# Expert blocks ordered by their first row's batch, with finished batches summed between the blocks

## The chip, the cores and the metric

The kernel runs on one core of one Trainium2 chip. The metric is device microseconds of one execution. Four runs of the kernel before gave a median of 751.23 us, between 750.31 and 752.97. A profile is one further execution with the hardware profiler on, and it has its own time.

The engines are written as in the profile: PE (TensorE), DVE (VectorE), ACT (ScalarE), POOL (GpSimd) and SP (SyncE, which here only issues DMAs). SPq, ACTq, POOLq are the engines' instruction queues.

## What is computed

One adaLN transformer block on x of 4 batches, 512 tokens each, 256 wide, in float32: a gated attention part and a gated mixture of experts. The part that matters here is the second one:

```python
h = _layernorm(x) * (1 + cb) + sb
cw = _combine_weights(h, gate_w)        # 4 of 16 experts per token, weights that sum to 1
out = 0
for e in range(16):
    a = _swiglu(h @ expert_up_w[e].T)   # 256 -> 2 x 176 -> 176
    out = out + cw[:, e:e + 1] * (a @ expert_down_w[e].T)
out = out + _swiglu(h @ shared_up_w.T) @ shared_down_w.T
x = x + gb * out                        # gb: a gate per batch and column
```

Only the 4 chosen experts of a token have a weight other than zero. The 2048 tokens give 8192 (token, expert) rows.

## The kernel before

**Routing.** `attention()` works through the batches in order. When a batch is done, the routing picks each token's four experts, and 16 indirect DMAs on POOL (L1342) write its rows into `rows_d` in DRAM. `rows_d` has a region of 2176 rows for each expert; a row holds the 256 values, the token's number and its 16 weights. `free` (16 numbers, L250) is where each expert's region is filled to; `slots` (L1325 to L1339) hands out the places and moves it on (L1333). Since batches are routed in order, the rows of an expert stand in the order of their batches.

**Table.** When all four batches are routed, `make_table` (L314) works out on DVE which 128 rows each of `NBLK` = 79 blocks takes: from the counts it gets the number of blocks per expert (L322, L329), the first block of each (L334, L338), and then, in five operations of 79 x 16 = 1264 columns on all partitions (L345, L352, L356, L365, L369), the expert and the row of every block. All partitions hold the same table; the blocks lie along the free axis, ordered by expert. SP and PE read a block's row and expert from partition 0 into a register (`read`, L388).

**Shared expert.** `shared` (L397) runs for all tokens around the table. Its up products are L416 on PE, L427 on ACT and L435, L436 on DVE; its down product is L454 on PE, then L464 on DVE (tile `o`, two buffers) and L470 on POOL, which adds it to `x_sb`.

**Blocks.** `block(j)` takes the rows of one block: `fetch` (L1493, a DMA issued by SP, into one of seven `x` buffers), `turn` (L1504, PE transposes), `copy` (L1509, ACT), `meta` (L1514 and L1517 on DVE: the token numbers, and the rows' weights for this expert, picked out with the table's `is_of` by a product and a reduce), `up` (L1524, PE), `silu` (L1534, ACT), `product` (L1538, DVE), `turn_back` (L1543, PE), `copy_back` (L1547, DVE), `down` (L1552, PE), `weigh` (L1562, ACT, into one of five `y_b` buffers), and `put` (L1565): an indirect DMA on POOL that adds the 128 rows to `acc_d` in DRAM by token. There are two arrays `acc_d`; block j adds to number j % 2, so a put waits for the put two blocks earlier.

**End.** After all blocks, the eight halves of batches are loaded from both arrays (L1613: one array on SP, one on ACT), added (L1618), multiplied by the gate (L1619), added to `x_sb` (L1623, on POOL and DVE in turn) and stored (L1624).

**What sets the order.** PE, DVE, ACT and SP run their instructions in the order in which `Plan` (L83) emits them. Every piece is added with an engine, a cost in us, its needs, and a due time; `Plan.next` takes the operation that can start first by these costs, and the lower due time among equals. `hold` models the buffers (`takes`, `gives`). The program then waits on semaphores for what each instruction reads and writes; DRAM tiles are tracked too, apart from `rows_d`. An engine's queue goes strictly in order.

Of the kernel before, what the change touches and what calls it, by code (L numbers as in the profile page):

```python
# [10 lines left out]
F32 = mybir.dt.float32  # L11
# [6 lines left out]
P = 128  # L18
# [18 lines left out]
CAP = B * S + P  # L37
NBLK = B * S * TOPK // P + E - 1
# [113 lines left out]
def kernel(  # L152
# [92 lines left out]
    tile_rows = steps_of("tile_rows", [P, B * NT], [[P, B * NT]])  # L245
    number = steps_of("number", [P, NBLK], [[1, NBLK]])
    expert = steps_of("expert", [P, E], [[1, E]])
    begin = steps_of("begin", [P, E], [[CAP, E]])

    free = const.tile([P, E], F32, name="free")  # L250
    nc.gpsimd.tensor_copy(free, begin)
# [59 lines left out]

    table = {}

    def make_table(pool, needs, due):  # L314
        t, n = table, NBLK

        def counts():

            rows = pool.tile([P, E], F32, name="rows", bufs=1)
            nc.vector.tensor_tensor(rows, free, begin, ALU.subtract)  # L320
            full = pool.tile([P, E, B * NT], F32, name="full", bufs=1)
            nc.vector.tensor_tensor(  # L322
                full,
                rows.unsqueeze(2).to_broadcast([P, E, B * NT]),
                tile_rows.unsqueeze(1).to_broadcast([P, E, B * NT]),
                ALU.is_gt,
            )
            t["blocks"] = pool.tile([P, E], F32, name="blocks", bufs=1)
            nc.vector.tensor_reduce(t["blocks"], full, AX.X, ALU.add)  # L329

        def starts():
            blocks = t["blocks"]
            earlier = pool.tile([P, E, E], F32, name="earlier", bufs=1)
            nc.vector.tensor_tensor(  # L334
                earlier, before, blocks.unsqueeze(1).to_broadcast([P, E, E]), ALU.mult
            )
            first = t["first"] = pool.tile([P, E], F32, name="first", bufs=1)
            nc.vector.tensor_reduce(first, earlier, AX.X, ALU.add)  # L338
            t["last"] = pool.tile([P, E], F32, name="last", bufs=1)
            nc.vector.tensor_tensor(t["last"], first, blocks, ALU.add)  # L340

        def of():

            t["gone"] = pool.tile([P, n, E], F32, name="gone", bufs=1)
            nc.vector.tensor_tensor(  # L345
                t["gone"],
                t["last"].unsqueeze(1).to_broadcast([P, n, E]),
                number.unsqueeze(2).to_broadcast([P, n, E]),
                ALU.is_le,
            )  # L350
            t["of"] = pool.tile([P, n], F32, name="of", bufs=1)
            nc.vector.tensor_reduce(t["of"], t["gone"], AX.X, ALU.add)  # L352

        def is_of():
            t["is_of"] = pool.tile([P, n, E], F32, name="is_of", bufs=1)
            nc.vector.tensor_tensor(  # L356
                t["is_of"],
                expert.unsqueeze(1).to_broadcast([P, n, E]),
                t["of"].unsqueeze(2).to_broadcast([P, n, E]),
                ALU.is_equal,  # L360
            )

        def base():

            nc.vector.tensor_tensor(  # L365
                t["gone"], t["is_of"], t["first"].unsqueeze(1).to_broadcast([P, n, E]), ALU.mult
            )
            t["row"] = pool.tile([P, n], F32, name="row_f", bufs=1)
            nc.vector.tensor_reduce(t["row"], t["gone"], AX.X, ALU.add)  # L369
            nc.vector.tensor_tensor(t["row"], number, t["row"], ALU.subtract)  # L370

        def rows():

            row, of = t["row"], t["of"]
            nc.vector.tensor_scalar(row, row, float(P), None, ALU.mult)
            nc.vector.scalar_tensor_tensor(row, of, float(CAP), row, ALU.mult, ALU.add)
            nc.vector.tensor_scalar(row, row, float(E * CAP), None, ALU.min)
            nc.vector.tensor_scalar(of, of, float(E - 1), None, ALU.min)
            for name in ("row", "of"):
                t[f"{name}_i"] = pool.tile([P, n], mybir.dt.int32, name=f"{name}_i", bufs=1)  # L380
                nc.vector.tensor_copy(t[f"{name}_i"], t[name])

        op = needs
        for f, cost in ((counts, 0.9), (starts, 0.9), (of, 2.8), (is_of, 1.4), (base, 2.8), (rows, 1.0)):
            op = plan.add("DVE", cost, f, needs=[op], due=due)
        return op

    def read(t, n, engine, top):  # L388
        return nc.values_load(
            t[0:1, n : n + 1],  # L390
# [97 lines left out]
    def attention():  # L488
        with ExitStack() as ectx:
# [665 lines left out]
            def norm2(b, adds, due):  # L1155
# [165 lines left out]
                def slots():  # L1321
# [7 lines left out]
                        free.unsqueeze(1).to_broadcast([P, NT, E]),  # L1329
# [3 lines left out]
                    nc.vector.tensor_tensor(free, free, pc[:, NT, :], ALU.add)  # L1333
# [100 lines left out]
    def ffn():  # L1434
# [5 lines left out]
        SP, PE = mybir.EngineType.SP, mybir.EngineType.PE  # L1440
# [19 lines left out]
        for b in range(EARLY_SHARED, B):  # L1460
# [5 lines left out]
            "DVE", 0.2, lambda: nc.vector.tensor_copy(ends, free), [routed[B - 1]["slots"]], 60.0  # L1466
        )

        def blanks(e):
            r = read(ends, e, SP, E * CAP - P)  # L1470
# [12 lines left out]
        def block(j):  # L1483
            st = {}
            due = 300.0 + j
            names = ("x", AHEAD + 1), ("pt2", 2), ("xt", 2), ("token", 6), ("pu", 2), ("sg", 2), \
                ("a_b", 2), ("pb", 1), ("at_b", 2), ("py", 2), ("y_b", 5)
            h = {name: hold(name, bufs) for name, bufs in names}

            def fetch():  # L1490
                r = read(t["row_i"], j, SP, E * CAP)
# [9 lines left out]
            def turn():  # L1501
# [3 lines left out]
                st["e"] = read(t["of_i"], j, PE, E - 1)  # L1505
# [4 lines left out]

            def meta():
                x = st["x"]
                st["token"] = fp.tile([P, 1], mybir.dt.uint32, name="token", bufs=6)
                nc.vector.tensor_copy(st["token"], x[:, D : D + 1])  # L1514
                st["cw"] = fp.tile([P, 1], F32, name="cw_b", bufs=6)
                junk = fp.tile([P, E], F32, name="junk")
                nc.vector.tensor_tensor_reduce(  # L1517
                    junk, x[:, D + 1 :], t["is_of"][:, j, :], 1.0, 0.0, ALU.mult, ALU.add, st["cw"]
                )
# [40 lines left out]
            def weigh():  # L1560
                st["y"] = fp.tile([P, D], F32, name="y_b", bufs=5)
                nc.scalar.activation(st["y"], st["py"], AF.Copy, scale=st["cw"])  # L1562

            def put():
# [12 lines left out]
            xt = plan.add("ACT", 0.37, copy, [op], due - 1.4, takes=[h["xt"]], gives=[h["pt2"]])  # L1577
            me = plan.add(
                "DVE", 0.4, meta, [fe, op], due - 0.3, takes=[h["token"]], gives=[h["x"]]
# [11 lines left out]
            )  # L1591
            op = plan.add("PE", 0.87, down, [op], due + 1.1, takes=[h["py"]], gives=[h["at_b"]])
# [3 lines left out]
            plan.add(  # L1596
                "POOL", 1.56, put, [op], due + 1.1, lag=4.0, gives=[h["y_b"], h["token"]]
            )

        for j in range(NBLK):  # L1600
            block(j)
# [5 lines left out]

        half = NT // 2
        sums = []
        for n in range(B * NT // half):  # L1610
            pair = [ep.tile([P, half, D], F32, name=f"s{n}_{i}") for i in range(2)]
            for t, acc, eng in zip(pair, acc_d, (nc.sync, nc.scalar)):
                eng.dma_start(  # L1613
                    out=t, in_=acc[ts(n, half * P), :].rearrange("(n p) d -> p n d", p=P)
# [70 lines left out]
```

## Time and profile before

| | |
|---|---|
| median of four runs | 751.23 us (750.31 to 752.97) |
| the profiled execution | 754.97 us |
| its span, first to last instruction | 753.0 us |
| granted PE clock, mean | 0.943 |
| busy: PE, DVE, ACT, POOL | 656.4, 455.6, 317.9, 347.1 us |

By stretch of the span (us from its start; busy us of each engine; the granted clock; the mean busy share of the 16 DMA engines):

| stretch | what runs | PE | DVE | ACT | POOL | PE clock | DMA |
|---|---|---|---|---|---|---|---|
| 50 to 430 | attention, routing of three batches | 353.87 | 286.06 | 206.82 | 171.60 | 0.97 | 0.24 |
| 430 to 463 | last batch, weights of the experts arrive | 28.53 | 19.54 | 4.88 | 12.07 | 0.97 | 0.87 |
| 463 to 488 | table, shared expert, last scatters | 12.42 | 14.69 | 1.42 | 18.48 | 0.75 | 0.65 |
| 488 to 536 | shared expert, first blocks | 47.52 | 20.14 | 11.55 | 13.27 | 0.96 | 0.23 |
| 536 to 717 | blocks | 181.00 | 66.30 | 84.12 | 112.33 | 1.00 | 0.67 |
| 717 to 726 | last blocks drain | 2.59 | 0.84 | 1.41 | 4.68 | 0.92 | 0.59 |
| 726 to 753 | sums and stores | 0.00 | 16.97 | 0.00 | 6.23 | 0.50 | 0.70 |

How to read the profile's lines. In a timeline a line is: start, duration, engine, source line, operation, out<-in, shapes, how many were merged (x), and in brackets how long the engine had been idle before and what released it. A group of a source line gives the count and the shortest, median and longest duration in ns, then the first and last start. "issue" as a releaser means that the profile shows nothing that the engine waited for. The ends of PE's operations are modelled.

### The profile page before, as it was taken

Reading aid. Unit: us, or ns where it says so; the run is one execution under the profiler, and the core shown is the slowest. Engines: PE = TensorE matmul, PEld = TensorE weight load, DVE = VectorE, ACT = ScalarE, POOL = GpSimd, SP = SyncE. Lnnn points to the kernel's source line nnn. Section 1 sums busy time; section 2 is a strip of 40 time slices with the busy share of each in tenths; the row PEclk is TensorE's granted clock in tenths of the full one; section 3 lists DMA queues with packets and bytes.
Section 4 is the critical chain, followed back from the end, with each engine's and each line's share of the span. In section 5 each row is a group of like instructions: output and inputs, shape, how many; then the busy total and the mean of one; then the engine's idle time right before and its main releaser. Section 6 shows DMA issues by size and latency. Waiting matters only on the chain.

```text
span 753.0 us, 12881 instructions
## 1 busy us (share of the span) xinstructions
PE 656.4 (87%) x4205; PEld 413.4 (55%) x4236; DVE 455.6 (61%) x1286; ACT 317.9 (42%) x557; POOL 347.1 (46%) x449
## 2 busy tenths in 40 slices
PE   6577999999999999999988895599999999999920
PEld 3343455554544544545543484488777777777710
DVE  4685868778887797787884067444333333333317
ACT  2103654575555655563655410013344444444400
POOL 4000222336257462673636553612566666666633
PEclk9687999999999999999998898799999999999975
DMA  4576211112133221332101295721567676677575
GB/s 133 128 238 206 70 28 40 41 41 52 28 102 101 57 64 25 100 95 56 42 18 54 90 291 204 177 58 23 89 108 111 109 112 112 105 114 109 58 186 183
DMA packets 54969, 74.51 MB, mean 99 GB/s; under 512 B 8024, under 2 KB 48056, under 8 KB 53752
## 3 DMA queue, kind: packets, MB, share of 16 engines
q1 hardware_dynamic: 37992, 51.99, 24.7%
q0 software_dynamic: 14448, 19.31, 16.0%
q10 hardware_dynamic: 2464, 2.39, 1.1%
q8 instruction: 35, 0.57, 0.3%
q14 instruction: 30, 0.25, 0.1%
HBM read 41.11 MB, written 32.16 MB: 97 GB/s over the span
## 4 chain that ended last, share of the span: by engine, by line
PE 64%; DVE 17%; DMA 8%; issue 3%; POOL 3%; ACT 2%; another core or an unknown queue 1%; SPq 1%; ACTq 0%; DVEq 0%; POOLq 0%
PE pu L1524 12%; PE py L1552 9%; PE pr L860 8%; PE pa L971 8%; PE p L1001 6%; DVE mx_s L881 6%; DMA down_sb<-in_down_t 4%; PE pu L416 3%; PE pr L868 3%; PE pb L1543 2%; PE pt L1504 2%; PE py L454 2%; PE p L580 2%; ACT ex L1013 1%; PE p L734 1%
## 5 line engine op out<-in xcount | busy, mean ns | idle before, releaser
L881 DVE TENSOR_REDUCE mx_s<-pr 128x1 f32<-128x384 f32 (+3 forms) x352 | 212.9, 636 | 53.2 <-PE pr L868 48.6
L1013 ACT ACTIVATE ex<-p 128x1024 f32<-128x1024 f32 (+1 forms) x192 | 163.4, 880 | 103.2 <-PE p L1001 74.0
L1020 POOL TENSOR_SCALAR_AFFINE_SELECT ex<-ex 128x256 f32<-128x256 f32 (+1 forms) x192 | 93.7, 495 | 181.0 <-ACT ex L1013 177.3
L1565 POOL DMA_INDIRECT acc_d<-y_b,token x79 | 123.0, 1557 | 77.1 <-DVE token L1514 58.2
L860 PE MATMUL pr<-kx,qx 125*128 125x384 bf16 (+3 forms) x512 | 125.1, 309 | 21.4 <-DVE mx_s L881 10.1
L1524 PE MATMUL pu<-up_sb,xt 128*128 x316 | 106.6, 460 | 0.0
L1001 PE MATMUL p<-qx,kx 128*128 128x384 bf16 (+3 forms) x481 | 92.5, 300 | 8.4 <-DMA qx<-mrow 5.9
L971 PE MATMUL pa<-ex,vaug 128*32 128x512 f32 (+3 forms) x1024 | 96.8, 450 | 2.3 <-POOL ex L1020 0.8
L860 PEld LDWEIGHTS <-qx 125*128 125x128 bf16 x512 | 46.8, 101 | 77.8 <-issue 58.6
L868 PE MATMUL pr<-seen,ident_h 128*128 128x128 bf16 (+2 forms) x352 | 88.4, 251 | 0.0
L1552 PE MATMUL py<-down_sb,at_b 88*128 x316 | 81.4, 379 | 1.2 <-DVE at_b L1547 1.2
L1538 DVE TENSOR_TENSOR a_b<-sg_b,pu 128x176 f32<-128x176 f32 x79 | 26.7, 338 | 90.5 <-issue 75.5
L1342 POOL DMA_INDIRECT rows_d<-row,slot x64 | 64.4, 1006 | 25.6 <-DVE slot L1339 13.0
L1552 PEld LDWEIGHTS py<-down_sb,at_b 88*128 88x128 f32 x316 | 59.7, 189 | 21.9 <-ACT y_b L1562 1.7
L1001 PEld LDWEIGHTS <-kx 128*128 128x128 bf16 x512 | 40.9, 98 | 40.7 <-issue 25.6
L1524 PEld LDWEIGHTS pu<-up_sb,xt 128*128 128x128 f32 x316 | 53.9, 190 | 16.8
L1562 ACT ACTIVATE y_b<-py,cw_b 128x256 f32<-128x256 f32 x79 | 37.5, 475 | 46.3 <-PE py L1552 46.3
L416 PE MATMUL pu<-h2t,sup_sb 128*128 128x256 f32 (+1 forms) x192 | 49.7, 409 | 5.7 <-DVE a L436 5.5
L1547 DVE COPY at_b<-pb 88x256 f32<-88x256 f32 x79 | 33.2, 421 | 32.3 <-PE pb L1543 31.8
L1534 ACT ACTIVATE sg_b<-pu 128x176 f32<-128x176 f32 x79 | 25.1, 318 | 60.5 <-PE pu L1524 60.5
L868 PEld LDWEIGHTS <-ident_h 128*128 128x128 bf16 x352 | 34.9, 99 | 22.8 <-issue 15.7
L416 PEld LDWEIGHTS pu<-h2t,sup_sb 128*128 128x128 f32 (+1 forms) x192 | 37.1, 197 | 14.6 <-DVE a L436 6.2
(176 smaller groups left out, 744.0 us busy)
## 6 DMA issues: line engine op xcount, KB each, us to landing
x<-rows_d SPq DMA_DIRECT2D x79, 136.5 KB
qx<-qd SPq DMA_DIRECT2D x48, 192.0 KB
up_sb<-in_up_t SPq DMA_DIRECT2D x8, 704.0 KB
acc_d<-blank SPq DMA_DIRECT2D x2, 2176.0 KB
qd<-pt SPq DMA_DIRECT2D x16, 192.0 KB
down_sb<-in_down_t SPq DMA_DIRECT2D x8, 352.0 KB
rows_d<-blank SPq DMA_DIRECT2D x17, 136.5 KB
x_sb<-in_x SPq DMA_DIRECT2D x4, 512.0 KB
```

What stands on the lines that cost most here:

```text
L416: nc.tensor.matmul(st["p"][:rows, w, :], lhsT=sup_sb[:, k, c0 : c0 + rows], rhs=h2t[:, k, c1 : c1 + half], start=(k == 0), stop=(k == KC - 1),
L860: nc.tensor.matmul(pr[:, h, :], lhsT=qx[s % 3][:QKZ, REP * j + r + h, ts(i, P)], rhs=kx[s % 3][:QKZ, j, :w], start=True, stop=False, skip_ ...
L868: nc.tensor.matmul(pr[:, :, w - P :], lhsT=ident_h, rhs=seen.unsqueeze(1).to_broadcast([P, n, P]), start=False, stop=True, skip_group_chec ...
L881: nc.vector.tensor_reduce(mx[s][:, i, c0 : c0 + n], st["pr"], AX.X, ALU.max)
L971: nc.tensor.matmul(st["pa"][32 * r : 32 * r + 32, c * P :], lhsT=vaugs[b % 2][:, c, SLOTS * n + j, :], rhs=exs[r], start=(j == 0 and c == ...
L1001: nc.tensor.matmul(pe[:, h, :], lhsT=kx[s % 3][:, j, ts(c, P)], rhs=qx[s % 3][:, REP * j + r + h, c * P :], start=True, stop=True,)
L1013: nc.scalar.activation(ex, st["pe"], AF.Exp, scale=qk_scale)
L1020: nc.gpsimd.affine_select(out=st["ex"][:, :, 0:P], in_=st["ex"][:, :, 0:P], pattern=[[0, n], [1, P]], base=0, channel_multiplier=-1, compa ...
L1342: dma = nc.gpsimd.indirect_dma_start(out=rows_d, out_offset=bass.IndirectOffsetOnAxis(ap=st["slot"][:, i, k : k + 1], axis=0), in_=st["row ...
L1524: nc.tensor.matmul(st["pu"], lhsT=st["xt"][:, k, :], rhs=up_sb[:, bass.ds(st["e"], 1), k, :].rearrange("p e f -> p (e f)"), start=(k == 0) ...
L1552: nc.tensor.matmul(st["py"], lhsT=st["at"][:, c, :], rhs=down_sb[:, bass.ds(st["e"], 1), c, :].rearrange("p e d -> p (e d)"), start=(c == ...
L1565: nc.gpsimd.indirect_dma_start(out=acc_d[j % 2], out_offset=bass.IndirectOffsetOnAxis(ap=st["token"][:, 0:1], axis=0), in_=st["y"], in_off ...
```

## The change

It has four parts.

1. **Order.** `free` becomes `upto`, of five rows: where each expert's region was filled to before each batch and after the last (L1333 writes the next row instead of moving one row on). With it the table orders the blocks by the batch of their first row, and by expert within that. There are 79 blocks as before.
2. **Table.** Partition j now holds block j, and along the free axis lie the 4 x 16 pairs of batch and expert. 25 DVE operations of 64 columns or fewer take the place of 18, among them a scan for the running sum. SP and PE read block j from partition j. As the table no longer has a row of `is_of` per block on every partition, DVE itself reads the block's expert into a register (`which`) and copies that column of the weights.
3. **Early sums.** Batch b is finished after block n - 1, where n = (b + 1) x 16 + 15. For each of the first three batches, when the program has come to block n + 14, `end` adds to the plan: four loads on SP (two halves from two arrays, 256 KB each), needing puts n - 2 and n - 1 and the copy-back of block n + 3; six DVE operations of 128x512, each after a further copy-back from block n + 8 on; and two stores on SP. `y_b` goes from five to eight buffers, `token` and `cw_b` from six to twelve.
4. **End.** After the blocks only the last batch is summed, in four tiles of 128x256, all on DVE.

In the changed kernel's order, the first batch's loads stand behind the fetch of block 43, the second's behind that of block 59, the third's behind that of block 75. The DVE operations of a batch stand behind the copy-backs of blocks 39 to 44, 55 to 60 and 71 to 76, one each.

```diff
-    free = const.tile([P, E], F32, name="free")
+    upto = const.tile([P, B + 1, E], F32, name="upto")
...
+        def begun():
+            rows, full = small("rows", [P, B, E]), small("full", [P, B, E])
+            nc.vector.tensor_tensor(rows, upto[:, 1:, :],
+                begin.unsqueeze(1).to_broadcast([P, B, E]), ALU.subtract)
+            nc.vector.tensor_scalar(rows, rows, 1.0 / P, 0.5 - 0.5 / P, ALU.mult, ALU.add)
+            nc.vector.tensor_scalar(full, rows, WHOLE, None, ALU.add)
+            nc.vector.tensor_scalar(full, full, WHOLE, None, ALU.subtract)
+        def order():
+            full, new, last = t["full"], small("new", [P, B, E]), small("last", [P, B * E])
+            nc.vector.tensor_copy(new[:, 0, :], full[:, 0, :])
+            nc.vector.tensor_tensor(new[:, 1:, :], full[:, 1:, :], full[:, : B - 1, :], ALU.subtract)
+            nc.vector.tensor_tensor_scan(
+                last, new.rearrange("p b e -> p (b e)"), zeros, 0.0, ALU.add, ALU.add)
...
         def of():
-            nc.vector.tensor_tensor(t["gone"],
-                t["last"].unsqueeze(1).to_broadcast([P, n, E]),
-                number.unsqueeze(2).to_broadcast([P, n, E]), ALU.is_le)
-            nc.vector.tensor_reduce(t["of"], t["gone"], AX.X, ALU.add)
+            nc.vector.tensor_scalar(gone, last, number, None, ALU.is_le)
+            nc.vector.tensor_reduce(of, gone, AX.X, ALU.add)
...
             def fetch():
-                r = read(t["row_i"], j, SP, E * CAP)
+                r = read(t["row_i"][j : j + 1, 0:1], SP, E * CAP)
...
+            def which():
+                st["e_v"] = read(t["of_i"][j : j + 1, 0:1], DVE, E - 1)
...
             def meta():
-                nc.vector.tensor_tensor_reduce(
-                    junk, x[:, D + 1 :], t["is_of"][:, j, :], 1.0, 0.0, ALU.mult, ALU.add, st["cw"])
+                nc.vector.tensor_copy(st["cw"], x[:, D + 1 :][:, bass.ds(st["e_v"], 1)])
...
+        def end(b, n, due):
+            needs = [*puts[n - 2 : n], backs[n + 3]]
+            pace = iter(backs[n + 8 :])
+            for n in range(NT // half):
+                holds = [hold(f"s{i}", 2) for i in range(2)]
+                def load(i, at=at, st=st):
+                    st[i] = fp.tile([P, half, D], F32, name=f"s{i}")
+                    nc.sync.dma_start(out=st[i], in_=acc_d[i][at, :].rearrange("(n p) d -> p n d", p=P))
+                def add(st=st):
+                    nc.vector.tensor_tensor(st[0], st[0], st[1], ALU.add)
+                def gate(st=st, b=b):
+                    nc.vector.tensor_tensor(
+                        st[0], st[0], g_sb[:, b, 1:2, :].to_broadcast([P, half, D]), ALU.mult)
+                def residual(st=st, tiles=tiles):
+                    nc.vector.tensor_tensor(st[0], st[0], x_sb[:, tiles, :], ALU.add)
+                def store(st=st, tiles=tiles):
+                    nc.sync.dma_start(out=out_r[:, tiles, :], in_=st[0])
+                op = [plan.add("SP", 0.5, lambda i=i, load=load: load(i), needs, due, takes=[holds[i]])
+                      for i in range(2)]
+                op = plan.add("DVE", 0.81, add, [*op, next(pace)], due, gives=holds[1:])
+                op = plan.add("DVE", 1.05, gate, [op, next(pace)], due)
+                op = plan.add("DVE", 0.7, residual, [op, next(pace)], due)
+                plan.add("SP", 0.5, store, [op], due, lag=4.0, gives=holds[:1])
+
+        puts = []
         for j in range(NBLK):
-            block(j)
+            puts.append(block(j))
+            for b in range(B - 1):
+                n = (b + 1) * S * TOPK // P + E - 1
+                if j == n + 14:
+                    end(b, n, 300.0 + n)
...
-        for n in range(B * NT // half):
-            pair = [ep.tile([P, half, D], F32, name=f"s{n}_{i}") for i in range(2)]
+        for n in range((B - 1) * NT, B * NT):
+            pair = [ep.tile([P, D], F32, name=f"s{n}_{i}") for i in range(2)]
...
-            eng = nc.gpsimd if n % 2 == 0 else nc.vector
-            eng.tensor_tensor(s, s, x_sb[:, ts(n, half), :], ALU.add)
+            nc.vector.tensor_tensor(s, s, x_sb[:, n, :], ALU.add)
```

## The prediction

> **What bounds the kernel now.** I read the page's chain of waits first (TensorE holds 64% of it, its largest lines L1524 and L1552, the expert blocks), then the busy time by stretch, then the timeline of each engine in the last 290 us. From 536 to 717 us TensorE is busy 181.00 of 181.00 us: the block stage is TensorE's, one block per 2.49 us. Two stretches are not TensorE's: the table that stops it ahead of the blocks, and the end. The table, in the timelines of VectorE and of TensorE:
>
> ```profile
> 465.75 1.47 DVE L345 TENSOR_TENSOR gone<-last,number 128x1264 f32<-128x1264 f32 x1
> ...
> 474.53 0.19 DVE L381 CAST of_i<-of 128x79 int32<-128x79 f32 x1
> 474.64 0.41 DVE L435 SCALAR_TENSOR_TENSOR t<-t,pu 96x256 f32<-96x256 f32 x1
> ```
>
> ```profile
> 475.56 1.22 PE L454 MATMUL py<-sdown_sb,a 96*128 96x256 f32 x2 [9.11 <-DVE t L435]
> ```
>
> The shared expert's product (L435) queues behind 11.1 us of table (463.51 to 474.64), and TensorE stands idle 9.11 us for it. The end, from the whole timeline:
>
> ```profile
> 722.18 1.55 POOL L1565 DMA_INDIRECT acc_d<-y_b,token  x1 [0.56 <-issue]
> 725.99 8.14 SPq L1613 DMA_DIRECT2D s<-acc_d  x8
> 732.08 0.69 DVE L1618 TENSOR_TENSOR s<-s,s 128x512 f32<-128x512 f32 x1 [12.52 <-DMA s<-acc_d]
> ...
> 734.13 1.63 DVE L1619 TENSOR_TENSOR s<-s,g_sb 128x512 f32<-128x512 f32 x1
> ...
> 748.84 0.69 DVE L1623 TENSOR_TENSOR s<-s,x_sb 128x512 f32<-128x512 f32 x1
> ```
>
> From the last put (722.18) to its landing 3.8 us (the load at 725.99 waits for it); from there to the end of the span, 753.0, another 27.0 in which TensorE does nothing.
>
> **Part 1, the table.** Out go 18 operations, five of them 1264 wide at 1.47 us. In come 25, 64 wide or less. Dependent 128x64 rows of the routing start 0.25 apart (456.56, 456.81), dependent 128x16 ones 0.2. 18 x 0.25 + 7 x 0.15 (those that need not wait) = 5.5 us. The scan has no row; a 128x64 reduce took 0.22, a 128x256 operation 0.42, so it is 0.2 to 0.5, and I take 0.3. VectorE is free 5.6 us earlier. What is late next is GpSimd: the third and fourth shared results need a buffer that GpSimd's L470 gives back, and L470 stands behind 16 scatters.
>
> ```profile
> 466.22 1.84 POOL L1342 DMA_INDIRECT rows_d<-row,slot  x1 [0.30 <-issue]
> 468.37 0.96 POOL L1342 DMA_INDIRECT rows_d<-row,slot  x1 [0.30 <-issue]
> ...
> 484.28 0.96 POOL L1342 DMA_INDIRECT rows_d<-row,slot  x1 [0.30 <-issue]
> 485.27 1.40 POOL L470 TENSOR_TENSOR x_sb<-x_sb,o 128x256 f32<-128x256 f32 x2
> ```
>
> In the changed order 30 matrix products of two rows of 0.215 each (12 of L416 take 2.59), 12.9 us, stand ahead of the one that needs that buffer. Started at 470.0 they end at 482.9, later if the granted clock stays low (0.61 in 466 to 476); L470 comes at 485.3, or near 483.7, since the three scatters longer than 0.96 lie beside the wide operations. So 0 to 3 us of the 5.6 go back into this wait. **-4.5**, bounds -2 and -6. Another 3.75 us of idle TensorE (484.7 to 488.5) has a releaser that the profile does not name; I give it neither way. The first fetch needs the scatters, not the table, and TensorE has shared work until 531.
>
> **Part 2, the end.** Eight halves become four tiles of 128x256, two-input operations of 0.42 (L436), 0.44 apart. From the landing of the last put: load issue to first sum 2.8 (bounds 2.2, a put's landing less its 1.55 on GpSimd, and 6.1, sixteen loads at once: 725.99 to 732.08), 12 x 0.44 = 5.3, then 3.4 from the last store's issue to the span's end as now (749.6 to 753.0): 11.5 in place of 27.0. GpSimd takes no part, so the 1.63 rows go too. **-15.5**, bounds -12 and -16.5.
>
> **Part 3, per block.** VectorE loads a register (L389) and copies one column in place of a reduce and its accumulator read (0.16 + 0.08). VectorE has no register load in this trace; the other sequencers do:
>
> ```profile
> L389 SPq TENSOR_LOAD <-row_i x79: 262/270/522, 480.0 to 693.6; - x79
> L389 PEldq TENSOR_LOAD <-of_i x79: 295/301/490, 498.5 to 710.6; - x79
> ```
>
> The gap it falls into:
>
> ```profile
> 656.93 0.34 DVE L1538 TENSOR_TENSOR a_b<-sg_b,pu 128x176 f32<-128x176 f32 x1 [1.18 <-ACT sg_b L1534]
> ```
>
> 1.18 us idle in every block takes 0.3, or 0.5 at its longest: **0**. In 18 blocks a sum operation (0.69) joins it: 0.69 + 0.3 + about 0.1 = 1.1, still inside by 0.1; at 0.5 it sticks out 0.1, 18 x 0.1 = 2 us, mostly hidden by part 4. The Trainium skill, "DMA: Bandwidth & Descriptors", Latency and other measured facts, gives such a load a floor of about 600 ns; the rows here say 270 and 301. By the page the 18 blocks would stick out 0.2 each, an estimated 3.7 us more.
>
> **Part 4, the puts.** This speaks against the change. Each early sum loads both arrays; the next put to an array waits for those loads, the loads for the two puts before (written into the built order: loads wait for puts 32 and 33, puts 34 and 35 for the loads; again 48/49 and 64/65). Put 33 starts 610.9, lands 3.8 later; load 3 is issued 0.45 after load 2 at 615.2, lands 3.2 later (between 2.2 and 6.1, a quarter of the way, four loads in place of sixteen); 0.6 to start the put (idle rows 0.30 to 0.77): put 34 at 619.0 instead of 613.4, **5.6 late**. How fast do puts catch up? GpSimd's timeline shows it after a hiccup:
>
> ```profile
> 648.23 1.55 POOL L1565 DMA_INDIRECT acc_d<-y_b,token  x1 [0.93 <-DVE token L1514]
> 651.53 1.56 POOL L1565 DMA_INDIRECT acc_d<-y_b,token  x1 [1.74 <-ACT xt L1509]
> 653.39 1.55 POOL L1565 DMA_INDIRECT acc_d<-y_b,token  x1 [0.30 <-ACT xt L1509]
> 656.15 1.56 POOL L1565 DMA_INDIRECT acc_d<-y_b,token  x1 [1.20 <-ACT xt L1509]
> ```
>
> GpSimd alone could go on every 1.86 us (651.53, 653.39), but the put two later, to the same array, started 4.62 after (656.15): it waits for the landing. Two blocks take 4.98, so a late put gains 0.18 a block. Put 34 to put 50: 7 x 4.62 + 1.9 + 3.8 + 0.45 + 3.2 + 0.6 = 42.3 against 16 x 2.49 = 39.8: 2.4 later per batch. Late at put 50: 8.0, at 66: 10.4, at 78: 10.4 - 1.4 = 9.0. Sum operations beside a put may lengthen it as the scatters were (0.96 to 1.84): 9 of the 18 on a chain by 0.25 adds 2. **+11**; bounds +1 (loads land in 2.2, puts 4.4 apart) and +20 (loads in 6.1). Eight y_b buffers cover 15 us of this, so TensorE need not wait, but the end waits for put 78. The Trainium skill, "SBUF — State Buffer", SBUF: two separate sides, says that a VectorE operation with two SBUF inputs and a GpSimd operation that reads SBUF shut each other out for a whole instruction. The scatters above agree in kind, though they grew by 0.25 to 0.88 beside operations of 1.47. With a full 0.69 on nine puts the estimate by the page would be +15.
>
> SP's fetches queue behind the waiting loads: fetch 44 about 6 us late, the last batch's (76) some 13 late with the puts. Seven x buffers hold 17 us less 3 for landing: **0**, cover 8 shrinking to 1. The first sum stands five blocks behind load 2, 4 us more than needed, at the last batch near none; up to 2 us of VectorE stall, hidden by the late puts. The constants' setup is narrower and lies ahead of any need: 0.
>
> **Sum**: -4.5 - 15.5 + 0 + 11 = -9.0, from 754.97 of the profiled execution (span 753.0 and 1.9 around it) 746.0. It lies 3.7 above the median of the four runs, 751.23; by that, **742.2**.
>
> **Rivals.** (A) Puts recover: loads land in 2.2 us and the lag stays under 5. For it: 1.86 between neighbours. Against it: 4.62 between every second. -4.5 - 15.5 + 4 = -16: 735. (B) The table gives nothing, because TensorE reaches the buffer wait sooner and the low clock stays, or the puts lag 14 to 17: -5 to -3, about 747. (C) Slower: VectorE's register load holds its queue for longer than the 1.18 us gap, in every block. An excess e moves the 33 blocks ahead of the first load by 33e, and the rest by 45e once that passes the lag of 11. It decides from e = 0.27 (33 x 0.27 = 9), a load of about 1.4 us; with e = 0.4: 13 + 7 - 9 = +11, 762. Against it: 0.27 and 0.30 in 158 rows. (D) The change does not do what it says: the loads wait for later puts, or the sums end behind the last put. The built order speaks against it.
>
> **Chances**: forecast (738 to 745) 0.56, A 0.15, B 0.16, C 0.09, D or nothing 0.04. The range leaves out C and the far ends: 733 to 750 (-18 and -1, near the bounds -4.5 - 15.5 + 1 and -2 - 15.5 + 17). Bound 0.3%, 2.25 us, about what a measurement tells from no change. Faster: the forecast, A and two thirds of B, 0.82; same: the rest of B and half of D, 0.07; slower: C and half of D, 0.11.
>
> **What would show it.** Right: L435 behind the table near 469 instead of 474.6; put 34 some 6 us behind its y_b and put 78 about 11 us after the last block's result; two puts to an array about 4.6 apart throughout; TensorE without gaps in the block stage; 11 to 12 us from last landing to end. Wrong: idle TensorE before L1543 with a VectorE releaser (C), idle before L1552 for y_b, or a put 78 on time (A).

## The result, and the profile after

The changed kernel takes 754.43 us (median of 52 runs) against 751.0 (median of 78 runs of the kernel before): ratio 1.0042, 95% interval 1.0029 to 1.0055. It is 0.4% slower; 742.2 was forecast. Its profiled execution has a span of 750.2 us. Executions scatter by some 5 us, and a good part of that lies ahead of the table, so the two profiles are compared from the last instruction of the routing (L1339, 463.12 before, 458.11 after). From there to the end: 289.9 us before, 292.1 after, +2.2, of a kind with the medians' +3.4.

| us after the routing's end | before | after | difference |
|---|---|---|---|
| first put | 59.87 | 58.48 | -1.4 |
| put 33 | 147.76 | 146.15 | -1.6 |
| put 78 | 259.06 | 277.32 | +18.3 |
| end of the span | 289.9 | 292.1 | +2.2 |
| from put 78 to the end | 30.87 | 14.76 | -16.1 |

**The table** is as short as forecast: 5.2 us instead of 11.2. The timelines of VectorE, then of TensorE, behind it:

```profile
463.54 0.15 DVE L381 CAST of_i<-of 128x1 int32<-128x1 f32 x1
463.62 0.41 DVE L435 SCALAR_TENSOR_TENSOR t<-t,pu 96x256 f32<-96x256 f32 x1
...
476.12 0.42 DVE L435 SCALAR_TENSOR_TENSOR t<-t,pu 128x256 f32<-128x256 f32 x1 [5.58 <-issue]
...
481.81 0.42 DVE L435 SCALAR_TENSOR_TENSOR t<-t,pu 128x256 f32<-128x256 f32 x1 [4.81 <-ACT t L427]
```

```profile
464.53 1.22 PE L454 MATMUL py<-sdown_sb,a 96*128 96x256 f32 x2 [2.86 <-DVE a L436]
...
477.05 3.31 PE L416 MATMUL pu<-h2t,sup_sb 128*96 128x256 f32 x8 [4.05 <-issue]
482.74 1.99 PE L416 MATMUL pu<-h2t,sup_sb 128*128 128x256 f32 x8 [2.39 <-DVE a L436]
```

TensorE's wait for L435 has shrunk from 9.11 to 2.86 us. But two waits follow, of 4.05 and 2.39, where the kernel before has one, of 3.75, and of the 6.25 won only 1.4 is left at the first put. That one wait of the kernel before, on TensorE and on ScalarE:

```profile
488.48 3.34 PE L416 MATMUL pu<-h2t,sup_sb 128*128 128x256 f32 x8 [3.75 <-DVE a L436]
```

```profile
487.13 0.65 ACT L427 ACTIVATE t<-pu 128x256 f32<-128x256 f32 x2 [5.33 <-remote]
```

TensorE's row does name its releaser, VectorE's L436. L436 stands behind L435 (487.55), and L435 behind ScalarE's tanh L427; only the row of L427 has a releaser that the profile cannot name ("remote").

**The puts** (GpSimd's timeline; the first line is put 33):

```profile
604.26 1.56 POOL L1565 DMA_INDIRECT acc_d<-y_b,token  x1 [0.94 <-DVE token L1517]
612.80 1.55 POOL L1565 DMA_INDIRECT acc_d<-y_b,token  x1 [6.98 <-DMA s<-acc_d]
614.66 1.56 POOL L1565 DMA_INDIRECT acc_d<-y_b,token  x1 [0.31 <-ACT xt L1509]
617.84 1.55 POOL L1565 DMA_INDIRECT acc_d<-y_b,token  x1 [1.62 <-DVE cw_b L1519]
...
650.70 1.56 POOL L1565 DMA_INDIRECT acc_d<-y_b,token  x1 [3.01 <-DVE a_b L1538]
658.83 2.13 POOL L1565 DMA_INDIRECT acc_d<-y_b,token  x1 [6.58 <-ACT y_b L1562]
661.27 2.19 POOL L1565 DMA_INDIRECT acc_d<-y_b,token  x1 [0.31 <-ACT y_b L1562]
664.60 1.55 POOL L1565 DMA_INDIRECT acc_d<-y_b,token  x1 [1.15 <-DVE token L1517]
669.66 1.56 POOL L1565 DMA_INDIRECT acc_d<-y_b,token  x1 [3.51 <-DVE cw_b L1519]
...
698.53 1.56 POOL L1565 DMA_INDIRECT acc_d<-y_b,token  x1 [1.09 <-DMA acc_d<-y_b,token]
707.32 2.08 POOL L1565 DMA_INDIRECT acc_d<-y_b,token  x1 [7.23 <-DVE a_b L1538]
...
735.43 1.55 POOL L1565 DMA_INDIRECT acc_d<-y_b,token  x1 [0.57 <-issue]
```

Three jumps are seen: 8.54 (put 33 to 34), 8.13 (49 to 50) and 8.79 us (65 to 66). Only the first has the load named as its releaser; the other two brackets name an engine that had long been done. From put 33 to put 78 it takes 131.2 us, where 45 blocks of 2.49 are 112.1: the last put is 19.1 late. In the third batch the lag reaches VectorE and TensorE (a timeline of each):

```profile
695.86 0.42 DVE L1547 COPY at_b<-pb 88x256 f32<-88x256 f32 x1 [0.40 <-PE pb L1543]
705.98 0.69 DVE L1623 TENSOR_TENSOR s<-s,s 128x512 f32<-128x512 f32 x1 [9.70 <-DMA s<-acc_d]
```

```profile
698.37 1.35 PE L1524 MATMUL pu<-up_sb,xt 128*128 x4
707.42 2.07 PE L1552 MATMUL py<-down_sb,at_b 88*128 x4 [7.71 <-DVE at_b L1547]
```

The first sum (L1623) waits 9.70 us for loads that wait for the late put 65; the copies of the blocks queue behind it, and TensorE stands idle for 7.71.

**The register load**, by line L389, VectorE's row (shortest, median, longest in ns):

```profile
L389 DVEq TENSOR_LOAD <-of_i x79: 304/315/1294, 465.4 to 707.0; - x79
```

Median 315, close to the 270 and 301 of the other queues; one of the 79 took 1.29 us. The Trainium skill's "DMA: Bandwidth & Descriptors", Latency and other measured facts, gives about 600 ns for it; the row decides.

### The profile page after: what moved, and what is told of

It reads as the page before. It is cut to its first block, busy times and chain, and to the rows that moved or that the text cites. A ratio compares the mean times of both kernels' runs of the same rounds, so it can differ in the third digit from the quotient of the medians.

```text
span 750.2 us, 12970 instructions
## 1 busy us (share of the span) xinstructions
PE 656.6 (88%) x4205; PEld 413.7 (55%) x4236; DVE 444.2 (59%) x1224; ACT 317.2 (42%) x557; POOL 342.8 (46%) x444
## 4 chain that ended last, share of the span: by engine, by line
PE 65%; DVE 12%; DMA 11%; issue 3%; POOL 3%; ACT 2%; SPq 2%; another core or an unknown queue 0%; ACTq 0%; DVEq 0%; POOLq 0%
PE pu L1524 12%; PE py L1552 9%; PE pa L971 8%; PE pr L860 8%; PE p L1001 6%; DVE mx_s L881 4%; DMA up_sb<-in_up_t 4%; PE pu L416 4%; DMA acc_d<-y_b,token 3%; PE pr L868 3%; PE pb L1543 2%; PE pt L1504 2%; PE py L454 2%; PE p L734 2%; PE p L580 2%
## 5 line engine op out<-in xcount | busy, mean ns | idle before, releaser
L1565 POOL DMA_INDIRECT acc_d<-y_b,token x79 | 126.7, 1604 | 97.3 <-ACT y_b L1562 22.2
L1342 POOL DMA_INDIRECT rows_d<-row,slot x64 | 62.8, 981 | 25.4 <-DVE slot L1339 12.8
```

The lines of the kernel that those rows point to most:

```text
L1342: dma = nc.gpsimd.indirect_dma_start(out=rows_d, out_offset=bass.IndirectOffsetOnAxis(ap=st["slot"][:, i, k : k + 1], axis=0), in_=st["row ...
L1565: nc.gpsimd.indirect_dma_start(out=acc_d[j % 2], out_offset=bass.IndirectOffsetOnAxis(ap=st["token"][:, 0:1], axis=0), in_=st["y"], in_off ...
```

## Experiments

The kernels ran in five groups, each on one chip with the kernel before: e1 to e4 on chip A, e5 to e8 on B, e9 to e12 on C, e13 to e16 on D, e17 and e18 on E. Ratios are to the kernel before on the same chip, with their 95% interval. The theory at the start was: the early loads make the puts wait, a late put recovers hardly at all, and nothing else is lost at the end.

**e1, e11, e15: the table alone, with the end of the kernel before.**

```diff
-                if j == n + 14:
+                if False:
                     end(b, n, 300.0 + n)
...
-        for n in range((B - 1) * NT, B * NT):
+        for n in range(B * NT // half):
...
```

> The new order, table and register load, with the end of the kernel before: no early sums, all four batches summed behind the last put. Theory (waits): the table's gain is mostly lost again ahead of the blocks, put 33 came only 1.6 us earlier against the routing's end, so about 751.0 - 1.6 = 749.4. The recorded prediction gave the table 4.5: 746.5. Rival (the new order or the register load costs something in every block): 751 or more.

Measured on three chips: 1.0023 (0.9995 to 1.0051), 1.0023 (0.9995 to 1.0050), 1.0034 (1.0009 to 1.0058). New order, table and register load together cost 1.7 to 2.5 us by these ratios (two of the three intervals reach no change), where 4.5 had been forecast as a gain and 1.6 by the theory. The blocks aren't the cause: from put 33 to put 78 e1 takes 111.5 us, the kernel before 111.3. The time is lost ahead of the first block.

> As e1 (new order and table, no early sums), now on the same chip as the changed kernel's repeat. Theory: 0.993 to 0.995 where the first block comes 49 us after the routing's end, 1.000 to 1.002 where it comes 60 after. It shows in either case what the table alone is worth, beside the changed kernel on one chip.

> As e1 and e11, the partner of e14. With slow register operations 1.002; without them 0.993.

**e2: no early sums** (the first `if` as in e1, the changed end kept; the sums and output rows of three batches are left out).

> The early sums left out altogether: the first three batches' sums and their output rows are not computed; the last batch is summed behind the last put as in the changed kernel. Theory (waits): no put lag is left, 751.0 - 1.6 - 16 = 733.4, put 78 within 1 us of its weighed result. If the lag of the puts has another cause than the early sums (order of the blocks, the register load), the time stays above 740 and the puts lag here too.

0.9806 (0.9764 to 0.9849). Put 78 starts 0.9 us after its weighed result. Against e1 on the same chip the shorter end gives 1.0023 - 0.9806 = 2.2%, 16.3 us, and the changed kernel's 1.0042 lies 2.4%, 17.7 us, above e2: that is what the early sums cost.

**e3: puts that do not wait for the early loads.** The loads read rows of a finished batch, the later puts write rows of later ones.

```diff
+                for l in early[j % 2]:
+                    tc.declare_no_dep(dma.ins, l, reason="later rows")
```

> The puts no longer wait for the early loads (they write rows of later batches); loads, sums and stores stay where they are. Theory (waits): the three jumps of 8 us between puts go, the loads land five blocks ahead of the first sum also in the third batch, VectorE's wait of 9.70 us and TensorE's of 7.71 go with them; puts at most 3 us late; 733.4 + 2 = 735. Rival (contention: transfers of 256 KB and sum operations draw the puts out, whoever waits): a lag of over 10 us remains, 745 or more.

0.9885 (0.9838 to 0.9932): 741.41 us, by the ratios 12 us below the changed kernel, 6 above the expectation. GpSimd's timeline from the same place, and SP's:

```profile
607.76 1.55 POOL L1565 DMA_INDIRECT acc_d<-y_b,token  x1 [0.93 <-DVE token L1517]
610.52 1.56 POOL L1565 DMA_INDIRECT acc_d<-y_b,token  x1 [1.20 <-ACT xt L1509]
612.74 1.55 POOL L1565 DMA_INDIRECT acc_d<-y_b,token  x1 [0.67 <-DVE token L1517]
617.31 1.56 POOL L1565 DMA_INDIRECT acc_d<-y_b,token  x1 [3.02 <-DVE a_b L1538]
619.17 1.55 POOL L1565 DMA_INDIRECT acc_d<-y_b,token  x1 [0.30 <-ACT sg_b L1534]
622.56 2.06 POOL L1565 DMA_INDIRECT acc_d<-y_b,token  x1 [1.83 <-ACT y_b L1562]
624.93 2.18 POOL L1565 DMA_INDIRECT acc_d<-y_b,token  x1 [0.30 <-ACT y_b L1562]
```

```profile
606.54 4.65 SPq L1620 DMA_DIRECT2D s<-acc_d  x4
611.78 9.51 SPq L1493 DMA_DIRECT2D x<-rows_d  x7
```

The jump at put 34 (607.76) is gone, and so are VectorE's and TensorE's waits. What stays is a hiccup behind each batch's loads: the loads hold the fetches back on SP, seven fetches follow at once, and the put at 610.52 took 6.04 us from start to landing where 3.8 is usual; that the fetches draw it out is read from the time at which they run, it was not tested. So the put two later to the same array starts at 617.31. With the longer puts behind it (2.06, 2.18) that adds 2 to 3 us per batch, and put 78 is 6.5 us late. So the theory holds for the larger part and the rival for the rest: the waits were worth 12 us, contention leaves 5 to 6.

**e4: early loads alone** (no sums, no stores; output rows of three batches left out).

```diff
-                op = plan.add("DVE", 0.81, add, [*op, next(pace)], due, gives=holds[1:])
-                op = plan.add("DVE", 1.05, gate, [op, next(pace)], due)
-                op = plan.add("DVE", 0.7, residual, [op, next(pace)], due)
-                plan.add("SP", 0.5, store, [op], due, lag=4.0, gives=holds[:1])
```

> Early loads issued, but not summed and not stored: the first three batches' output rows are not computed. The puts wait for the loads as in the changed kernel. Theory (waits): the put lag is nearly that of the changed kernel, 16 to 20 us at put 78, time 750 to 754, although VectorE never waits for a load. Rival (the sum operations, VectorE's wait and the stores make the lag above the forecast 11): put 78 11 us late or less, 741 to 745.

1.0000 (0.9971 to 1.0030). From put 33 to put 78 126.8 us, 14.7 late: a little under the 16 expected. With sums and stores it is 19.1 in the profile above, but 14.1 and 19.3 in two more profiles of the changed kernel (e10 and e13). So the loads alone make most of the lag, and what sums and stores add to it can't be told from one profile each; by the ratios (1.0000 against 1.0042) they add some 3 us. TensorE is idle here too, in the third batch, for another reason: fetch 76 stands behind the waiting loads on SP.

```profile
710.43 0.69 PE L1504 MATMUL pt<-ident,x 128*128 128x128 f32 x2 [3.83 <-DMA x<-rows_d]
```

**e8, e12: the sum operations two blocks later.**

```diff
-            pace = iter(backs[n + 8 :])
+            pace = iter(backs[n + 10 :])
...
-                if j == n + 14:
+                if j == n + 15:
```

> As the changed kernel, but the sum operations stand two blocks later on VectorE (behind copy-backs 41, 57 and 73). VectorE's wait for the third batch's loads falls from 9.7 to about 4.7, TensorE's from 7.7 to about 3. Theory (the puts set the end, and TensorE's wait lies beside them): no change, 753 to 755. Rival (TensorE's wait is the loss): 5 us faster, 749 to 750.

0.9953 (0.9928 to 0.9978) on chip B, where the changed kernel itself did not run: as if the rival were right. So the pair was run once more on one chip.

> The changed kernel, unchanged, beside the kernel before on the same chip. Theory: where the first block comes 49 us after the routing's end the table brings 4.5, and the change ends even or 2 us faster (ratio 0.997 to 1.000); where it comes 58 to 60 after, the table brings 0 to 1.6 and the ratio is 1.002 to 1.006 as first measured. Rival (the table has no part in it): 1.004 on either.

> As e8, on the same chip as the changed kernel. Theory (the puts set the end, TensorE's wait lies beside them): the same ratio as the changed kernel within 0.2%. Rival (TensorE's wait of 7.7 us is part of the loss): lower by 0.5% or more.

On chip C the changed kernel has 1.0048 (1.0019 to 1.0077) and this one 1.0047 (1.0018 to 1.0076), though VectorE's longest wait for the loads is down from 5.37 us (e10) to 0.53. TensorE's idle time there is not shorter: 3.72 us behind fetch 76 in place of 3.38 behind VectorE. So that TensorE's wait costs nothing is not tested by this pair; it is read from put 78, which starts 10.5 (e10) and 10.0 us (e12) behind its weighed result: the puts set the end, and they are later than TensorE. The gain in e8 goes with the chip.

**e6, e7, e16: three accumulators**, alone (e6), and with puts free of the loads (e7, e16).

```diff
-    acc_d = [scratch.tile([B * S + P, D], F32, name=f"acc_d{n}") for n in range(2)]
+    acc_d = [scratch.tile([B * S + P, D], F32, name=f"acc_d{n}") for n in range(3)]
...
-                    out=acc_d[j % 2],
+                    out=acc_d[j % 3],
...
+                op = plan.add("DVE", 0.81, lambda add=add: add(i=2), [op, next(pace)], due, gives=holds[2:])
```

> Three accumulators in turn instead of two (a third array is zeroed, loaded and added; the end has 16 sum operations for 12); puts still wait for the loads. Theory (a late put is held by the landing of the put before it to the same array): puts now follow each other at 1.86 and gain 0.6 a block; jumps of 8 to 10 us remain, each made good before the next load; put 78 is under 3 us late, the end 2 us longer: 739. Rival (the lag stays because transfers or VectorE hold GpSimd): put 78 10 us late or more, 750 or more.

0.9955 (0.9929 to 0.9981), 742.17 us: 3 us over the expectation's 739, and that on a chip where the kernel before takes only 744.87. GpSimd's timeline, from put 33:

```profile
602.28 1.55 POOL L1565 DMA_INDIRECT acc_d<-y_b,token  x1 [0.94 <-ACT y_b L1562]
613.68 1.55 POOL L1565 DMA_INDIRECT acc_d<-y_b,token  x1 [9.85 <-DMA s<-acc_d]
...
621.93 2.18 POOL L1565 DMA_INDIRECT acc_d<-y_b,token  x1 [0.30 <-ACT y_b L1562]
624.42 2.19 POOL L1565 DMA_INDIRECT acc_d<-y_b,token  x1 [0.30 <-ACT y_b L1562]
626.91 2.19 POOL L1565 DMA_INDIRECT acc_d<-y_b,token  x1 [0.30 <-ACT y_b L1562]
...
634.38 1.55 POOL L1565 DMA_INDIRECT acc_d<-y_b,token  x1 [0.31 <-ACT y_b L1562]
636.24 1.55 POOL L1565 DMA_INDIRECT acc_d<-y_b,token  x1 [0.30 <-issue]
638.10 1.55 POOL L1565 DMA_INDIRECT acc_d<-y_b,token  x1 [0.30 <-issue]
```

Two things are seen. Free of the same array, puts do follow each other at 1.86 (634.38, 636.24, 638.10): the landing had held the recovery, as the theory says. But puts beside a sum operation take up to 2.19 instead of 1.55, and 2.19 + 0.30 is 2.49, the pace of the blocks: six such puts follow each other in the first batch, and over them there is no recovery. It depends on when the operation starts. The six have theirs 0.08 us after the put's start; put 34 of the first batch and put 66 of the third, with one 0.86 and 0.58 us after it, took 1.55. The first jump is also longer, 11.4 us, with six loads ahead of it instead of four. Put 78 is 6.1 us late.

> Both: puts don't wait for the early loads, and three accumulators. Theory: no jumps, and what landings are drawn out beside loads, stores and fetches is made good at once; put 78 under 2 us late, 736 + 2 = 738, below e3 (741.4). Rival (what e3 still loses isn't in the recovery of the puts): no better than e3, with the longer end 743.

> As e7, on the same chip as the changed kernel: puts free of the loads, three accumulators. Theory: put 78 under 2 us late, 2.0% below the changed kernel (19 us of lag less 2 for the longer end and less what the lag of TensorE was worth, 15 to 17). Rival (e7's gain was its chip's): less than 1% below.

e7: 0.9835 (0.9798 to 0.9872), put 78 within 0.6 us of its result, and 9 us below e6 on the same chip. e16: 0.9968 (0.9942 to 0.9993) on chip D, beside the changed kernel's 1.0045 (1.0014 to 1.0076): 0.8% below it, by the letter the rival's figure. From the routing's end the profile of e16 is 17 us shorter than that of e13 (277.6 against 294.7), but that end comes at 465.5 us instead of 458.4.

**e17, e18:** e3 again, and e7 with the third array zeroed later:

```diff
+                if s == 6:
+                    plan.add("SP", 3.0, lambda: blank_sums(acc_d[2:]), [*third, loaded[s][-1]], s)
```

> As e3, beside e18 on one chip: puts free of the loads, two accumulators. Theory: 0.986 to 0.990, as first measured, 1.5% below the changed kernel's 1.0045.

> As e7 and e16, but the third array is zeroed in the middle of the attention stage instead of at its beginning, where in e16 the routing's end came at 465.5 us instead of 456 to 461. Theory (the third array's 2 MB of zeroes beside the first loads cost 5 us there): routing's end at 460 or earlier, 0.985, no worse than e17. Rival (the accumulator's cost lies elsewhere): 0.996 as e16.

e17: 0.9783 (0.9740 to 0.9826), 729.91 us. e18: 0.9764 (0.9726 to 0.9803), 728.14 us, with the routing's end at 460.75. e7 and e18 both take 266.2 us from the routing's end to the end of the span, and e18's routing ends 4.0 us earlier than e7's: as far as two profiles from two chips can show it, the zeroing at the beginning was the loss ahead of the blocks. Much of the two low ratios goes with chip E: e17 is the kernel of e3, and its first result comes 49.4 us after the routing's end instead of 60.2. Both versions beat the kernel before; which of the two is the better is not told apart. Neither ran beside the changed kernel; e3 and the changed kernel have ratios of 0.9885 and 1.0042 to the same kernel before.

**e5, e9, e13, e14: where the table's gain goes.** e5 and e14 compute the whole table twice.

```diff
-        for f, cost in ((begun, 0.9), (order, 0.8), (place, 0.7), (of, 0.9), (rows, 2.0)):
+        for f, cost in ((begun, 0.9), (order, 0.8), (place, 0.7), (of, 0.9), (rows, 2.0)) * 2:
```

> As e1 (new order and table, end as before), with the whole table computed a second time, 5.3 us more on VectorE ahead of the shared product L435. Theory (the products behind the table run slowly until some 10 us after the routing's end, whatever the table does): the first block starts as before, 59 to 61 us after the routing's end, time within 1 us of e1's 752.6. Rival (the recorded reasoning: each us of table costs about 0.8 us at the blocks): 756 to 757.

> The kernel before, unchanged, for a profile on the same chip as the next three. In e6 to e8 the first block's result came 49.3 us after the routing's end, in the changed kernel's first profile 57.7, with the same table; e5 with a table 5.05 us longer 53.2. Theory (the chip of e5 to e8 lets TensorE run at full clock behind the table, and there the table's 6 us count about 0.8 each): before 53 to 55 here if this is such a chip, 59 if it is like the first. Rival (the table is worth nothing anywhere): no more than 1.5 above the changed kernel's figure on the same chip.

> The changed kernel beside its table variants and the best version on one chip. Theory (slow sequencers): where SP's register operations take 0.7 us between 6 and 23 us after the routing's end, the table brings nothing: first block 58 to 60 after it, ratio 1.004. Where they stay at 0.05, first block 49 after it, and the ratio is that of e8, 0.995. Rival (the difference between the chips has to do with something else): a fast first block beside slow register operations, or the reverse.

> The table computed twice, end as before, on the same chip as the single table of e15. Theory (slow sequencers): with slow register operations within 1 us of e15 (the time until 23 us after the routing's end is lost anyway); without them 3.9 us slower than e15, as the first block came 53.2 against 49.3 us after the routing's end. Rival (each us of table costs 0.8 everywhere): 4 us slower than e15 in either case.

| chip | kernel | routing's end to table's end, us | first result after the routing's end, us | ratio |
|---|---|---|---|---|
| B | e8, one table | 5.4 | 49.3 | 0.9953 |
| B | e5, two tables, end as before | 10.5 | 53.2 | 0.9981 (0.9959 to 1.0003) |
| C | e9, kernel before | 11.4 | 56.6 | |
| C | e10, changed kernel | 5.4 | 60.1 | 1.0048 |
| D | e15, one table, end as before | 5.4 | 60.0 | 1.0034 |
| D | e14, two tables, end as before | 10.5 | 60.7 | 1.0051 (1.0026 to 1.0077) |

e5's and e1's times can't be set side by side, as they come from two chips; the first block can. On chip B 5.05 us of table more cost 3.9 at the first block. On D they cost 0.6 at the first block, where the rival asked for 4; the time, 0.17% or 1.3 us more, has too wide an interval to decide alone. On C the shorter table comes with a first block 3.4 us later, which neither theory had expected. Most of that is seen in TensorE's rows (e9, then e10):

```profile
479.81 1.99 PE L416 MATMUL pu<-h2t,sup_sb 128*128 128x256 f32 x8 [1.83 <-DVE a L436]
481.64 1.46 PE L454 MATMUL py<-sdown_sb,a 128*128 128x256 f32 x6
```

```profile
484.34 3.78 PE L416 MATMUL pu<-h2t,sup_sb 128*128 128x256 f32 x8 [5.12 <-DVE a L436]
487.92 2.23 PE L454 MATMUL py<-sdown_sb,a 128*128 128x256 f32 x6
```

Both go on at the same place of TensorE's queue, 24.6 (e9) and 24.5 us (e10) after the routing's end. But e9 had waited there for 1.83 us and goes on with the granted clock at 1.00 (26 to 30 us after the routing's end), e10 for 5.12 and goes on at 0.55: the fourteen products take 6.01 us instead of 3.45, which is 2.6 of the 3.4. Counting the first profile and those from A, C and D, nine of eleven with the short table have this slow stretch (0.54 to 0.59), and their first result at 60.0 to 60.2; the other two have the clock at 1.00 there, and 57.7 and 57.8. The kernel before has 59.1 in its first profile, with 0.59 there, and 56.6 in e9. With the clock at 1.00 there, the short table's first result is still some 1 us later than the long one's, for which the runs give no cause.

The sign that goes with the chips is in SP's queue. Its register instructions at L1471, in the changed kernel's first profile and in e8 (shortest, median, longest in ns):

```profile
L1471 SPq FUSED_REGOPS  x16: 3/37/717, 459.3 to 485.3; - x16
L1471 SPq MOVE rows_d<-blank x16: 3/33/702, 459.4 to 485.3; - x16
```

```profile
L1471 SPq FUSED_REGOPS  x16: 37/37/51, 460.1 to 475.0; - x16
L1471 SPq MOVE rows_d<-blank x16: 29/29/43, 460.2 to 475.1; - x16
```

A register move takes 0.03 us; in the first profile single ones take 0.70, and SP needs until 485.3, 27 us after the routing's end, for what it does in 16 in e8. The two profiles shown first and all from chips A, C and D have such instructions, between 6 and 23 us after the routing's end (in the kernel before from 16 us on), and their first result comes 56.6 to 60.7 us after it; those from B and E have none, and it comes at 49.3 to 53.2. They are a sign and not shown to be the cause: e12 has a single one and e11, on the same chip, seven, and both have their first result at 60.0. In the same stretch ScalarE's tanh (L427) starts late, without a releaser in the profile or behind one that had long been done. Its second start behind the table lies 23.1 to 23.4 us after the routing's end in every profile with the short table from A, C and D, and at 23.2 and 24.0 in the two of the kernel before; e6, e7, e8, e17 and e18 have it at 14.8 to 14.9. (In e14, with two tables, it is the first that starts at 23.1.) So on those chips a stage that ends 23 us after the routing takes up whatever the table gives. It isn't the profiler's doing: e8 and e12 are the same kernel, their profiles differ by 11.5 us from the routing's end to the span's end (278.8 and 290.3), and their medians without it by 11.55 (741.35 and 752.90). What makes the instructions slow, and why on these chips only, stays open. The stretch is that of the 16 scatters, the last of which starts 19.6 us after the routing's end; that is a coincidence in time, no more.

## Why the prediction was wrong

**Part 1, the table (-4.5, measured +1.7 to +2.5 with the order): failed.** The table's length, L435's place behind it and TensorE's shorter wait were right. The step that failed is "0 to 3 us of the 5.6 go back into this wait", a wait for GpSimd's L470, while the 3.75 us of idle TensorE were given "neither way". In the changed kernel's profile TensorE's second wait (2.39 us) ends at 482.74 behind ScalarE's tanh at 481.39, and L470 had ended at 480.08. The 3.75 us were the mark of the stretch that takes the gain up: on chips A, C and D what reached it earlier waited there, and mostly went on at a lower clock, for which the sum had no term. The prediction also read that the profile names no releaser for the 3.75; TensorE's row names L436, and only the row of the tanh behind it has none. Why the tanh is late stays open. Where that stretch is missing (chip B) two tables against one cost 0.77 us per us, and 6.0 us less would bring 4.6, an estimate from e5 and e8 that agrees with the 4.5; no kernel before was profiled there.

**Part 2, the end (-15.5): right.** 30.87 to 14.76 us from the last put's start, -16.1; -16.3 from e1 and e2.

**Part 3, the register load (0): right.** Median 315 ns, one of 79 at 1.29 us, blocks at 2.49 us, the 45 blocks from put 33 in e1 0.2 us longer than before.

**Part 4, the puts (+11, measured 19.1 against the pace of 2.49; 19.7 against the kernel before, from the first put to the last): the mechanism was right, a term was mis-sized.** The three jumps were forecast at 8.1 us and measured 8.54, 8.13 and 8.79. What failed is the step "a late put gains 0.18 a block". That is an undisturbed pair's figure (4.5 to 4.6 in the traces), and beside the early sums few pairs are undisturbed. From put 34 to 49, forecast to gain 3.1 on the schedule, 0.55 was lost; from 50 to 65, forecast to gain 3.1, another 2.35; from 66 to 78, forecast 1.4 (12 blocks at 0.18 would be 2.2, a slip in the prediction's sum), 1.8 were won. With 1.3 from the jumps that is 10.0 us more, against 2 allowed for sum operations. Three things are seen where it was lost: landings drawn out to 7.64 (put 51) while the seven fetches run that the waiting loads had held back; puts of up to 2.19 us beside sum operations; and a hiccup at put 49 that is there without any sums (3.70 in e2, 4.57 in the changed kernel). e6 takes the same-array landing away and shows the second alone. Of the lengthening, 0.25 a put had been allowed on nine puts; up to 0.64 was measured, on eight puts 3.7 us in all. How much is lost between the jumps differs between executions of the same kernel: from put 34 to 65, apart from the jump at 50, 2.9 in this profile, 4.0 in e13, while e10 gained 0.3. The gain of 6.2 that was forecast there is in none of them; the jumps (7.8 to 8.8) and the gain from put 66 on (1.6 to 2.4) are of a kind in all three. The lag is 14.1 in e10 and 19.3 in e13. The Trainium skill's "SBUF — State Buffer", SBUF: two separate sides, with its lock for a whole instruction, was nearer here for puts that start with the operation: the operation takes 0.68, and 0.64 of it shows in put 51. For an operation that starts later the lock does not show: put 67 has one 0.60 us after its start, and took 1.56.

**Fetches (0) and VectorE's stall (2 us, hidden): hidden as said, but not in size.** VectorE waited 9.70 us and TensorE 7.71; in e4 and e12 TensorE waited 3.83 and 3.72 for fetch 76. Put 78 started 10.0 us behind its weighed result, so the late puts cover it.

**The rivals.** B (table gives nothing, lag of 14 to 17) was the nearest in kind, but put at 747, since it let only one of the two go all the way. Both terms failed in the same direction: -1.4 - 16.1 + 19.7 = +2.2, in the profile, at the places of the sum -4.5 - 15.5 + 11. C, with a register load of over 1.18 us in every block, did not happen.

## What to carry to other kernels

A recovery rate read off one hiccup in a quiet stretch is a best case; work out how much of the stretch after the change is still quiet, transfers and neighbours' operations included. An idle stretch whose chain of releasers ends at one that the profile does not name, close behind the wait that one means to shorten, is the first candidate to take the gain up. And a load of a finished part should not make the writers of other parts wait: saying so to the dependency tracking was worth 12 us here.

## What the runs showed of the hardware that was not expected

On three of the five chips of the experiments, register instructions of SP's queue took 0.6 to 0.7 us, in five profiles one of them 1.4, instead of 0.03, in the stretch from 6 to 23 us after the routing's end; on the other two none did. The same kernel has a ratio of 0.9953 on one of the latter and 1.0047 on one of the former. An indirect put of 128x256 took 2.19 us instead of 1.55 beside a VectorE operation of 0.68 with two SBUF inputs that started within 0.1 us of it, and 1.55 where the operation started 0.5 to 0.9 us after it. On TensorE the granted clock stayed at 1.00 behind a wait of 1.83 us (e9) and was 0.55 behind one of 5.12 (e10). The routing's end came at 464.5 to 465.5 us in the three profiles with a third array of 2.2 MB zeroed at the beginning (e6, e7, e16), at 455.2 to 463.7 in those with two arrays, and at 460.75 with the zeroing moved.
